# A perceiver layer with routed tokens and experts on one core: ranks and counts of the token sort moved into the batches, the planner's clock in its last steps, and pairs of states added in the last scan

## The chip, the core and the metric

The kernel runs on one core of one Trainium2 chip. The metric is the time on the device in microseconds (us), the median of several runs. TensorE (PE, with its weight loads shown apart as PEld), VectorE (DVE), ScalarE (ACT), GpSimd (POOL) and SyncE (SP, which only issues transfers here) each execute their own queue in the order in which the program issues it; they wait for one another by semaphores. All data are float32.

## The reference, cut to what matters

B = 4 batches of T = 256 tokens with D = 256 features are the state x; each batch has a context of S = 4096 rows. Three parts are added to x one after the other:

```python
x = x + cross_attention(layernorm(x), ctx)     # 8 heads of 64; keys: the context and the tokens themselves
x = x + token_router(layernorm(x))             # see below
x = x + experts(layernorm(x))                  # 8 experts, 2 for each token

# token router, for each batch
scores = gelu(xn @ r_w1 + r_b1) @ r_w2 + r_b2
top 64 of 256 tokens  -> a small attention among them
other 192, in order   -> a state space scan: 512 channels, 16 states
    h[t] = dA[t] * h[t-1] + dBu[t];   y[t] = sum over 16 states of h[t] * C[t]

# experts
routing = softmax(xf @ router_w.T); the two largest, divided by their sum, weigh
out = sum over the two experts e of  w_e * ((silu(x @ gate_e) * (x @ up_e)) @ down_e)
```

So the experts of a batch's tokens are known only when that batch's scan has ended, and the scan of a batch needs that batch's cross attention.

## The kernel before

**Cross attention** fills the first 1264 us. It runs in N = 128 steps, 32 for a batch, and two further turns of the loop drain it (`for n in range(N + 2)`, from L1406). A group G is two heads of one batch, eight steps. In a step, PE multiplies the scores `su` (`scores`, L1247 to L1261); VectorE copies them out with their maximum (`copy_max`, L1273, L1280) and finds the common bound `nb` after a small product (`stat`, L1285, L1290); ACT takes the exponentials of the step before (`exps`, L1301); VectorE transposes these (`turn`, L1310, two a step, for the two heads). Every four steps PE multiplies the transposed blocks with the values (`values`, L1319, `po`), which have to wait for the last of the four pairs of transposes. The keys and values of the next group, `psk` (L1200) and `psv` (L1237), are multiplied in between as "pieces". The last pieces of a group's own tokens (`psv` again) and the output projection `psx` (`project`, L1366), added to x on VectorE (L1374), end each batch. The last steps have no pieces: there is no next group.

**The planner.** The program text is executed once, when the kernel is built, and writes out each engine's queue. Work that is not attention lies in background generators. `slot(budget)` is called at fixed places of a step; it lets every active generator that is due by the clock `now[0]`, and whose announced cost fits into what is left of the budget, go on to its next `yield due, cost`. The clock is an estimate: it moves by fixed amounts as pieces and scores are issued.

```python
def slot(budget):
    room[0] = budget
    for item in list(active):
        if item[1] <= now[0] and item[2] <= room[0]:
            room[0] -= item[2]
            step(item)
```

A smaller first number after `yield` lets the generator be continued at an earlier slot; the costs are guesses of VectorE's time.

**The background** is, for each batch after its attention (`routed`): router, small attention (`attention`; its softmax yields at L429), the scan's preparation, the scan, `ssm_back` (sums, output product `pssd`, `psback` that puts the rows in place). For batches 0, 1 and 2 `ssm_scan` runs beside the attention of the batch that follows, with POOL taking part of it. Then `sortable(b)` (L841 to L880) normalizes the batch's tokens: moments on VectorE, `x4` on ACT (L851), a transfer to `x4d` in memory (L855), four transposes `psx4` on PE (L863), copies `x4T` on ACT (L869), the logits `pslg` on PE (L874), and their copy to `lgs` on VectorE (L878).

After batch 2, `dispatch` (L907 to L1027) sorts the 768 tokens of the first three batches (NSORT = 6 tiles of 128) to their experts, all at once: `ranks` (L882 to L890) finds each expert's place among a token's eight logits by comparing all with all; `weights_of` (L892 to L905) has the marks of the two chosen ones, an exponential on ACT, and the two weights; a running sum over the six tiles (L936 to L938); three matmuls `pscnt` that count over partitions (L943 to L949); the number of blocks of 128 for each expert and where they begin (L954 to L960); each token's `slots` (L967 to L973) and `weights` in one loop; `experts`, the expert of each of the NB = 19 blocks (L977 to L982); each token's block and place in it (L991 to L995); then the comparisons `inb` (L1003, L1006) and `at` (L1012), 12 x 2 products `pstok` on PE (L1022) and the cast to `tokens` (L1026), the list of rows that each block gathers. In the queues, these operations stand among the operations of the last steps of the attention.

**The expert stage.** `ordered` runs the 19 blocks: for block j an indirect transfer on POOL's queue gathers the 128 rows of x4d that `tokens` names (`gather`, L1567), the expert's three matrices are loaded on SP's queue by the number in `experts` (`load`, L1529), PE transposes the rows (`turn_block`, L1579, copied by ACT at L1582) and multiplies gate and up (`half`, p0b and p1b, L1588), ACT takes a tanh and VectorE gates (`gated`, L1538 to L1543: `sg`, `hb`), PE multiplies down (`pdb`, L1602), and the rows go to `ysd` in memory (L1610). The pools of gathered rows and of expert weights lie in the memory that the attention used before. Beside these blocks run router, small attention and scan of the last batch, batch 3. Its scan is `ssm_scan_late` (L677 to L751): 16 parts of 4 states x 128 channels x 192 tokens. For each part ACT computes four decays, VectorE multiplies (L738), scans (L739) and multiplies by C (L745), and PE adds the four states by four products with the identity, accumulated in one bank `yps` (`sums`, L711 to L717):

```python
def sums(i):
    k, m = divmod(i, NDT)
    for s in range(SG):                       # SG = 4
        nc.tensor.matmul(
            yps[:, m // 2, (m % 2) * NBOT : (m % 2 + 1) * NBOT], ident, dbl[i][:, s, :],
            start=False, stop=(k == K - 1 and m % 2 == 1 and s == SG - 1),
        )
```

`ssm_back` (L754) and `prepare` (L1661) end that batch's routing; `collect` gathers the experts' rows of the first three batches and adds them with the `weights`; and the last batch goes through all eight experts densely (`experts`, pg and pu L1719, pde L1732).

Of the kernel before, what the change touches and what calls it, by code (L numbers as in the profile page):

```python
# [8 lines left out]
F32 = mybir.dt.float32  # L9
# [37 lines left out]
def perceiver_layer(ctx: ExitStack, tc: tile.TileContext, a: dict, out: bass.AP):  # L47
# [311 lines left out]
    def attention(b, st):  # L359
# [69 lines left out]
        yield 2.5, 0.9  # L429
# [248 lines left out]
    def ssm_scan_late(b, st):  # L678
# [32 lines left out]
        def sums(i):  # L711
            k, m = divmod(i, NDT)
            for s in range(SG):
                nc.tensor.matmul(
                    yps[:, m // 2, (m % 2) * NBOT : (m % 2 + 1) * NBOT], ident, dbl[i][:, s, :],
                    start=False, stop=(k == K - 1 and m % 2 == 1 and s == SG - 1),
                )  # L717
# [16 lines left out]
        for i in range(K * NDT):  # L734
# [10 lines left out]
            nc.vector.tensor_tensor(db, db, spread[k, 1], ALU.mult)  # L745
            if i:
                sums(i - 1)
# [80 lines left out]
    lgs = bg.tile([P, NSORT, E], F32, name="lgs")  # L828
# [12 lines left out]
    def sortable(b):  # L841

        yield 1.5, 1.2
# [14 lines left out]
        yield 2.5, 0  # L858
# [13 lines left out]
        for t in range(2):  # L872
# [5 lines left out]
        nc.vector.tensor_copy(  # L878
            lgs[:, 2 * b : 2 * b + 2, :].rearrange("p t e -> p (t e)"), ps[:, : 2 * E]
        )  # L880
# [26 lines left out]
    def dispatch():  # L907

        n = NSORT
        yield 1.7, 1.1  # L910
        gt, eq = scratch(0, [P, n, E, E], "gt"), scratch(1, [P, n, E, E], "eq")
        parts = [scratch(i, [P, 2 * DS * DTR * 3 // 4], "part") for i in range(2)]
        used = [0, 0]
# [13 lines left out]
        rk, comb, two = carve(0, n, E), carve(0, n, E), carve(0, n, E)  # L927
        mx, sm = carve(0, n), carve(0, n)
        for _ in ranks(lgs, n, rk, gt, eq):
            yield 1.0, 1.3  # L930
        yield 1.0, 1.0
        w = weights_of(lgs, rk, comb, two, mx, sm)
        next(w)

        prev = carve(0, n + 1, E)
        nc.vector.memset(prev[:, 0, :], 0.0)  # L936
        for t in range(n):
            nc.vector.tensor_tensor(prev[:, t + 1, :], prev[:, t, :], two[:, t, :], ALU.add)  # L938
        yield 2.0, 1.0
        next(w, None)  # L940
        ps = bank("pscnt")
        cnt, num = ps[:, : n * E], ps[:, n * E : (n + 1) * E]
        nc.tensor.matmul(  # L943
            cnt, cs["tri"], two.rearrange("p t e -> p (t e)"), start=True, stop=False
        )
        nc.tensor.matmul(
            cnt, ones, prev[:, :n, :].rearrange("p t e -> p (t e)"), start=False, stop=True
        )
        nc.tensor.matmul(num, ones, prev[:, n, :], start=True, stop=True)  # L949
        yield 1.7, 1.1  # L950

        full, nblk = carve(0, E, n), carve(0, E)
        bb, sb = carve(1, E, E), carve(0, E)
# [3 lines left out]
        nc.vector.tensor_reduce(out=sb, in_=bb, axis=AX.X, op=ALU.add)  # L957

# [5 lines left out]
        mine, sl = carve(1, 2, n, E), carve(0, 2, n)  # L964
        for dst, src in ((sl, slot), (order["weights"], comb)):
            for k in range(2):
                nc.vector.scalar_tensor_tensor(  # L967
                    out=mine[:, k], in0=rk, scalar=float(k), in1=src,
# [3 lines left out]
            if src is slot:  # L972
                nc.vector.tensor_copy(order["slots"], sl.rearrange("p k t -> p (k t)"))  # L973
                yield 1.0, 1.0

        end, past, eb = carve(0, E), carve(1, NB, E), carve(1, NB)
        nc.vector.tensor_tensor(end, sb, nblk, ALU.add)  # L977
        nc.vector.tensor_tensor(
            past[:1], bc(end[:1], 1, NB), bc(cs["iblk"][:1], 2, E), ALU.is_le
        )  # L980
        nc.vector.tensor_reduce(out=eb[:1], in_=past[:1], axis=AX.X, op=ALU.add)
        nc.vector.tensor_scalar(  # L982
            out=order["experts"], in0=eb[:1], scalar1=float(E - 1), scalar2=None, op0=ALU.min
        )
# [25 lines left out]
        for i, tag in enumerate(("ua", "permT", "dsort")):  # L1010
# [6 lines left out]
            if i == 1:  # L1017
                yield 1.0, 0.7
# [783 lines left out]
```

## Time and profile before

| | us |
|---|---|
| median of 3 runs (1548.88 to 1555.13) | 1551.75 |
| the profiled execution | 1554.27 |
| its span in the trace | 1552.5 |
| PE busy | 1468.3 (95% of the span) |
| PEld busy | 1048.7 (68%) |
| DVE busy | 1045.3 (67%) |
| ACT busy | 757.0 (49%) |
| POOL busy | 410.0 (26%) |

The mean clock granted to PE is 0.979 of full; 223.40 MB are moved, 144 GB/s on the mean. By stages, the busy times are (from the trace cut into stretches):

| stretch, us | what | length | PE | DVE | ACT | granted clock |
|---|---|---|---|---|---|---|
| 586 to 893 | middle of the attention | 307.0 | 299.4 | 232.5 | 174.1 | 1.00 |
| 1200 to 1264 | last steps of the attention, dispatch | 64.0 | 49.7 | 42.0 | 20.5 | 0.87 |
| 1264 to 1350 | first blocks, router of batch 3 | 86.0 | 71.3 | 28.1 | 35.3 | 0.88 |
| 1350 to 1457 | blocks, last scan, its output | 107.0 | 98.9 | 76.8 | 37.6 | 0.97 |
| 1457 to 1552 | experts of the last batch | 95.0 | 86.7 | 44.3 | 15.7 | 0.98 |

How to read such a profile: the span is the time from the first to the last instruction of the execution; the time of a run is a little longer. "Busy" counts an engine's instructions and not its waits. A line L1310 is line 1310 of the kernel. In groups and timelines, `pt<-sp` means a tile pt written from a tile sp, then shapes, the number of instructions, and in brackets the idle time of the engine before it and the instruction that ended that wait. A wait printed as `PE x L1 <- DMA y: 4.7, 3, 2.5` lists the total, the number and the longest. The chain of waits follows the last instruction back to what released it, step by step.

### The profile page before, as it was taken

The page shows a single profiled execution, that of the slowest core. Times are in us where ns is not written, and L with a number is a line of the kernel's source. Part 1 is how long each engine was busy: PE and PEld are TensorE (multiplying, and loading weights), DVE is VectorE, ACT ScalarE, POOL GpSimd, SP SyncE. Part 2 cuts the span into 40 slices and gives each one's busy share as a digit, 9 for nine tenths or more (in the row PEclk, how much of TensorE's full clock was granted, in tenths as well). Part 3 has the DMA queues.
Part 4 walks back from the last instruction along what each step waited for, and adds up shares of the span by engine and source line. Part 5 has one row for each costly group of instructions (what it writes and reads, how often), then busy time and mean ns, then how long its engine had stood idle before and what let it go on. Part 6 is the DMA issues. An engine that isn't in the chain of part 4 may idle for free.

```text
span 1552.5 us, 37355 instructions
## 1 busy us (share of the span) xinstructions
PE 1468.3 (95%) x15748; PEld 1048.7 (68%) x15748; DVE 1045.3 (67%) x1771; ACT 757.0 (49%) x1483; POOL 410.0 (26%) x464
## 2 busy tenths in 40 slices
PE   7999999999999899999999999999998779799899
PEld 3757667576667475776665667756666558688787
DVE  1666666666599976565999755758987644477453
ACT  3444454464566644545667454556654422534211
POOL 1000000000089940000799500006995011010110
PEclk9999999999999999999999999999999969999999
DMA  7445543524344525243454343335543144667562
GB/s 235 155 131 160 164 142 101 180 75 141 116 149 142 178 87 189 82 141 109 141 171 160 110 154 116 108 113 156 166 130 107 37 139 128 230 218 244 157 208 83
DMA packets 157766, 223.40 MB, mean 144 GB/s; under 512 B 14976, under 2 KB 76160, under 8 KB 157600
## 3 DMA queue, kind: packets, MB, share of 16 engines
q1 hardware_dynamic: 152368, 211.45, 42.5%
q10 hardware_dynamic: 3744, 5.51, 1.1%
q0 software_dynamic: 1488, 4.07, 1.0%
q8 instruction: 124, 2.03, 0.5%
q14 instruction: 42, 0.34, 0.1%
HBM read 216.56 MB, written 4.42 MB: 142 GB/s over the span
## 4 chain that ended last, share of the span: by engine, by line
PE 67%; POOL 14%; DVE 10%; issue 4%; ACT 2%; DMA 2%; ACTq 0%; SPq 0%; DVEq 0%; POOLq 0%
PE po L1319 12%; PE su L1253 11%; PE psv L1237 11%; PE psk L1200 10%; POOL y L652 5%; POOL db L637 5%; POOL db L650 4%; DVE sp L1273 4%; PE su L1261 2%; PE pg L1719 2%; PE pde L1732 2%; PE pu L1719 2%; PE p0b L1588 2%; PE p1b L1588 2%; DVE db L644 1%
## 5 line engine op out<-in xcount | busy, mean ns | idle before, releaser
L1273 DVE TENSOR_SCALAR_CACHE_REDUCE sp<-su 128x1088 f32<-128x1088 f32 x256 | 318.8, 1281 | 182.0 <-PE su L1261 182.0
L1310 DVE STREAM_TRANSPOSE pt<-sp 128x1088 f32<-128x1088 f32 x256 | 328.0, 1296 | 62.8 <-PE po L1319 62.6
L1301 ACT ACTIVATE sp<-sp,nb 128x1088 f32<-128x1088 f32 x256 | 305.2, 1196 | 10.6 <-DVE nb L1290 10.4
L1319 PE MATMUL po<-pt,v 128*64 128x128 f32 x4352 | 261.7, 277 | 1.3 <-DVE pt L1310 1.3
L1253 PE MATMUL su<-kt,qz 64*32 64x512 f32 x4096 | 255.1, 607 | 4.3 <-DVE nb L1290 3.5
L1200 PE MATMUL psk<-ctx,wk 128*128 128x512 f32 x512 | 246.3, 614 | 8.9 <-DMA ctx<-in_ctxT 6.4
L1237 PE MATMUL psv<-wv,ctx 128*128 128x128 f32 x2048 | 250.3, 279 | 0.2
L1319 PEld LDWEIGHTS po<-pt,v 128*64 128x64 f32 x4352 | 240.0, 138 | 12.8 <-issue 7.5
L1237 PEld LDWEIGHTS psv<-wv,ctx 128*128 128x128 f32 x2048 | 236.1, 192 | 6.3 <-issue 1.5
L1200 PEld LDWEIGHTS psk<-ctx,wk 128*128 128x128 f32 x512 | 91.7, 192 | 93.9 <-issue 86.7
L1188 ACT COPY kt<-psk 128x512 f32<-128x512 f32 x128 | 74.8, 585 | 158.5 <-PE psk L1200 158.3
L1253 PEld LDWEIGHTS su<-kt,qz 64*32 64x32 f32 x4096 | 63.2, 107 | 123.5 <-issue 93.3
L652 POOL TENSOR_TENSOR y<-y,db 128x192 f32<-128x192 f32 x192 | 135.0, 703 | 15.1
L1241 ACT COPY v<-psv 128x512 f32<-128x512 f32 x144 | 78.9, 558 | 118.4 <-PE psv L1237 117.2
L644 DVE TENSOR_TENSOR_SCAN db<-da,db 128x384 f32<-128x384 f32 x96 | 123.2, 1283 | 14.4 <-POOL db L637 3.7
L650 POOL TENSOR_TENSOR db<-db,cb 128x384 f32<-128x384 f32 x96 | 110.5, 1152 | 26.4 <-DVE da L642 26.4
L395 POOL TENSOR_TENSOR kbd<-qk,hmask 128x512 f32<-128x512 f32 x8 | 8.2, 1044 | 407.6 <-ACT qk L385 407.6
L637 POOL TENSOR_TENSOR db<-bb,xc 128x384 f32<-128x384 f32 x96 | 111.0, 1178 | 0.2
L1261 PEld LDWEIGHTS su<-kt,qz 128*32 128x32 f32 x2048 | 34.7, 110 | 109.3 <-issue 109.3
L632 ACT ACTIVATE da<-delta,A_log_sb 128x192 f32<-128x192 f32 x192 | 75.4, 447 | 51.5 <-DVE da L642 39.1
L1356 ACT COPY ao<-po 128x128 f32<-128x128 f32 x32 | 8.5, 264 | 165.5 <-PE po L1319 165.5
L1285 PEld LDWEIGHTS su<-mq,same 128*128 128x128 f32 x256 | 40.7, 190 | 53.6 <-DVE mq L1280 36.3
(277 smaller groups left out, 1594.0 us busy)
## 6 DMA issues: line engine op xcount, KB each, us to landing
ctx<-in_ctxT SPq DMA_DIRECT2D x256, 512.0 KB, 4.8
gateT<-in_gateT SPq DMA_DIRECT2D x27, 512.0 KB, 4.0
upT<-in_upT SPq DMA_DIRECT2D x27, 512.0 KB, 5.3
downT<-in_downT SPq DMA_DIRECT2D x27, 512.0 KB, 6.2
bb<-bcd SPq DMA_DIRECT2D x24, 192.0 KB, 4.1
cb<-bcd SPq DMA_DIRECT2D x24, 192.0 KB, 3.6
wv<-in_wv SPq DMA_DIRECT2D x32, 128.0 KB, 2.4
in_w<-in_in_w SPq DMA_DIRECT2D x32, 128.0 KB, 3.9
```

The source lines that it names most:

```text
L637: nc.gpsimd.tensor_tensor(db, bbs[k], bc(xc[:, m, :], 1, SG), ALU.mult)
L644: nc.vector.tensor_tensor_scan(out=db, data0=da, data1=db, initial=0.0, op0=ALU.mult, op1=ALU.add,)
L650: nc.gpsimd.tensor_tensor(db, db, cbs[k], ALU.mult)
L652: nc.gpsimd.tensor_tensor(y[:, m, :], y[:, m, :], db[:, s, :], ALU.add)
L1200: nc.tensor.matmul(ps, wqk[G][:, 0, c, :], ct[:, c, :], start=(c == 0), stop=(c == KD - 1),)
L1237: nc.tensor.matmul(ps[:, i * P : (i + 1) * P], lhsT, wv[G][:, w, c, :], start=(c == 0), stop=(c == KD - 1),)
L1241: nc.scalar.copy(v.rearrange("p k d -> p (k d)"), ps[:, : n * P])
L1253: nc.tensor.matmul(su[q * 32 : (q + 1) * 32, SC[j] + lo : SC[j] + lo + 512], qT[r, j, s * 32 : (s + 1) * 32], kt[r, q, lo : lo + 512], sta ...
L1273: nc.vector.tensor_scalar(out=sps[n][j], in0=su[:, SU[j] : SU[j] + QK], scalar1=1.0, scalar2=None, op0=ALU.mult, op1=ALU.max, accum_out=nm ...
L1301: nc.scalar.activation(sps[n][j], sps[n][j], AF.Exp, bias=nbs[n][:, j : j + 1], accum_out=lss[b][:, hp, s, j : j + 1],)
L1310: nc.vector.transpose(pts[m, j][:, i, :], sps[n][j])
L1319: nc.tensor.matmul(pos[m][j * HD : (j + 1) * HD, :], vts[m // 2, k // 4][:, k % 4, j * HD : (j + 1) * HD], pts[m, j][:, :, kk * 32 : (kk + ...
```

## The change

Four things are changed.

1. *Ranks, weights and counts by batch.* `sortable(b)` no longer keeps the logits; after the logits' product it copies them, ranks them, marks the chosen two, takes the exponential on ACT and adds the marks to the running sum `upto`, for its two tiles alone, at one slot. The rest of the weights follows at another slot for batches 0 and 1 and is left for later for batch 2. `dispatch` begins with the count products, now four of them.
2. *The order in dispatch.* The blocks' experts are found directly after the counts, ahead of the slots; the three comparisons `at` each have a slot; the weights of batch 2 and the choice of all `weights` come last, after `tokens`.
3. *The planner.* Due times are changed at four places (1.5 to 1.0, 2.5 to 1.7, 2.5 to 4.0 and those of dispatch). In the last steps (`tail`) the clock also moves for the pieces that are missing there, and one slot's budget is 1.3 instead of 0.5.
4. *The last scan.* VectorE adds the two pairs of states of a part in one further operation (128 x 384 elements), and `sums` has two products a part instead of four.

```diff
@@ attention
-        yield 2.5, 0.9
+        yield 4.0, 0.9
@@ ssm_scan_late
         def sums(i):
             k, m = divmod(i, NDT)
-            for s in range(SG):
+            for s in range(SG // 2):
                 nc.tensor.matmul(
                     yps[:, m // 2, (m % 2) * NBOT : (m % 2 + 1) * NBOT], ident, dbl[i][:, s, :],
-                    start=False, stop=(k == K - 1 and m % 2 == 1 and s == SG - 1),
+                    start=False, stop=(k == K - 1 and m % 2 == 1 and s == SG // 2 - 1),
                 )
...
             nc.vector.tensor_tensor(db, db, spread[k, 1], ALU.mult)
+            nc.vector.tensor_tensor(db[:, : SG // 2], db[:, : SG // 2], db[:, SG // 2 :], ALU.add)
             if i:
                 sums(i - 1)
@@ sortable
-        yield 1.5, 1.2
+        yield 1.0, 1.2
...
-        yield 2.5, 0
+        yield 1.7, 0
         ps = bank("psx4")
...
-        nc.vector.tensor_copy(
-            lgs[:, 2 * b : 2 * b + 2, :].rearrange("p t e -> p (t e)"), ps[:, : 2 * E]
-        )
+        yield 1.0, 1.25
+
+        part, used = scratch(0, [P, 384], "part"), 0
...
+        nc.vector.tensor_copy(lg, ps[:, : 2 * E])
...
+        for _ in ranks(lg, 2, rks[:, tiles], gt, eq):
+            pass
+        w = weights_of(lg, rks[:, tiles], combs[:, tiles], twos[:, tiles], mx, sm)
+        next(w)
+        for t in range(2 * b, 2 * b + 2):
+            if t:
+                nc.vector.tensor_tensor(
+                    upto[:, t, :], upto[:, t - 1, :], twos[:, t, :], ALU.add
+                )
+            else:
+                nc.vector.tensor_copy(upto[:, 0, :], twos[:, 0, :])
+        if b < B - 2:
+            yield 1.7, 1.0
+            next(w, None)
+        else:
+            order["weigh"] = w
@@ dispatch
-        for _ in ranks(lgs, n, rk, gt, eq):
-            yield 1.0, 1.3
-        yield 1.0, 1.0
-        w = weights_of(lgs, rk, comb, two, mx, sm)
-        next(w)
...
+        yield 1.7, 0
+
         ps = bank("pscnt")
         cnt, num = ps[:, : n * E], ps[:, n * E : (n + 1) * E]
+        for t0, t1, last in ((0, 1, True), (1, n, False)):
+            nc.tensor.matmul(
+                cnt[:, t0 * E : t1 * E], cs["tri"],
+                twos[:, t0:t1].rearrange("p t e -> p (t e)"), start=True, stop=last,
+            )
         nc.tensor.matmul(
...
+            cnt[:, E:], ones, upto[:, : n - 1].rearrange("p t e -> p (t e)"),
+            start=False, stop=True,
+        )
+        nc.tensor.matmul(num, ones, upto[:, n - 1, :], start=True, stop=True)
+        yield 1.7, 1.25
...
+        nc.vector.tensor_reduce(out=eb[:1], in_=past, axis=AX.X, op=ALU.add)
+        nc.vector.tensor_scalar(
+            out=order["experts"], in0=eb[:1], scalar1=float(E - 1), scalar2=None, op0=ALU.min
+        )
+
         slot = carve(0, n, E)
...
+        yield 1.0, 1.25
+        chosen(sl, slot)
+        nc.vector.tensor_copy(order["slots"], sl.rearrange("p k t -> p (k t)"))
...
-        yield 1.0, 1.2
-
+        yield 1.0, 1.25
+
...
-        yield 1.0, 1.3
 
         ats = []
         for i, tag in enumerate(("ua", "permT", "dsort")):
+            yield 1.0, 0.7
             at = bg.tile([P, 4, P], F32, tag=tag, name="at")
...
             ats.append(at)
-            if i == 1:
-                yield 1.0, 0.7
         yield 1.5, 0.2
         ps = bank("pstok")
...
         nc.vector.tensor_copy(order["tokens"], ps[:, :NB])
         order["ready"] = True
+        yield 1.0, 1.25
+        next(order["weigh"], None)
+        chosen(order["weights"], combs)
@@ main loop
+                tail = n >= N - 2
+
                 def piece(i):
                     if i < len(pieces):
                         pieces[i]()
+                    if i < len(pieces) or tail:
                         now[0] += took
...
-                    slot(0.5)
+                    slot(1.3 if tail else 0.5)
```

`chosen(dst, src)` is the former loop over slots and weights as a function: for k = 0, 1 it multiplies (rank equal to k) with src and sums over the experts.

## The prediction

> **What bounds the kernel now.** I read the page's chain first, then the stretches of ten microseconds over the end, then the chain in order of time and the waits of each stage.
>
> ```profile
> PE 67%; POOL 14%; DVE 10%; issue 4%; ACT 2%; DMA 2%; ACTq 0%; SPq 0%; DVEq 0%; POOLq 0%
> ```
>
> The page has PE busy 95% of the span, and PE holds 67% of the chain. Between 586 and 893 us the waits of PE add up to 7.4 us, so there its order decides. The end is another stage:
>
> ```profile
> 1220.00:1230.00 10.00, 8.95 (x156) 7.01 (x155) 6.50 (x13) 2.64 (x5) 0.00 (x0) 1.00 0.01 3
> 1230.00:1240.00 10.00, 5.46 (x55) 2.28 (x55) 6.56 (x19) 2.72 (x5) 0.00 (x0) 0.66 0.00 1
> 1240.00:1250.00 10.00, 2.76 (x19) 2.04 (x20) 9.24 (x22) 2.48 (x4) 0.00 (x0) 0.66 0.00 0
> 1250.00:1260.00 10.00, 9.49 (x82) 7.72 (x78) 5.74 (x22) 0.00 (x0) 0.00 (x0) 0.82 0.01 2
> 1260.00:1270.00 10.00, 8.05 (x93) 7.29 (x93) 2.83 (x11) 3.29 (x7) 0.77 (x1) 0.86 0.49 165
> 1270.00:1280.00 10.00, 6.70 (x24) 5.03 (x25) 0.00 (x0) 3.96 (x7) 5.30 (x7) 0.50 1.05 365
> ```
>
> Columns: stretch, length, busy time of PE, PEld, DVE, ACT, POOL, granted clock, DMA share, GB/s. From 1230 to 1250 VectorE (15.8 of 20 us) sets the pace and PE is idle or at half clock; from 1270 PE waits for transfers. The timeline shows what opens the expert stage:
>
> ```profile
> 1263.81 0.40 SPq L1529 DMA_DIRECT2D gateT<-in_gateT  x1
> ...
> 1268.18 0.18 DVE L1026 CAST tokens<-pstok 128x19 int32<-128x19 f32 x1 [0.88 <-PE pstok L1022]
> ...
> 1269.23 1.12 POOL L1567 DMA_INDIRECT xg<-x4d,tokens  x1 [78.22 <-DMA upT<-in_upT]
> ...
> 1276.82 3.79 PE L1588 MATMUL p0b<-xTb,gateT 128*128 128x128 f32 x16 [0.46 <-ACT xTb L1582]
> ```
>
> The last value product ends at 1263.77 (T below). The experts were known at 1252.5, yet the weights start at T: their memory is the attention's. Only the gather is later, by 5.4 us, because of the tokens. Then the scan stage:
>
> ```profile
> PE p0b L1588 <- DMA gateT<-in_gateT: 4.7, 3, 2.5
> PE yps L714 <- DVE db L745: 2.9, 3, 2.0
> ```
> ```profile
> DVE sg L1539 <- ACT sg L1538: 19.9, 8, 5.9
> ```
> ```profile
> 1368.16 0.95 DVE L738 TENSOR_TENSOR db<-bbl,xc 128x768 f32<-128x768 f32 x1
> 1369.15 1.76 DVE L739 TENSOR_TENSOR_SCAN db<-dal,db 128x768 f32<-128x768 f32 x1
> 1370.94 0.96 DVE L745 TENSOR_TENSOR db<-db,cbl 128x768 f32<-128x768 f32 x1
> 1371.82 0.95 DVE L738 TENSOR_TENSOR db<-bbl,xc 128x768 f32<-128x768 f32 x1
> ```
>
> Waits of 1349 to 1457 (PE) and 1349 to 1446 (VectorE): total, times, longest. PE has 7.6 us of large waits in 100 us, VectorE 19.9. So the last scan is PE's, and VectorE has 20 us to give; one scan costs it 3.66 us (1368.16 to 1371.82).
>
> **A. Up to the last value product.** The built order of the changed kernel shows what moves.
> A1. In steps 61, 93 and 125 the transposes psx now stand ahead of the own-token products psv (1.14 us). These filled PE's wait for ACT's first x; now PE waits there (1212.8 to 1213.7), waits 0.70 for the second x as before, and runs psv after it. The next scores start 1.0 later: +3.0 in all; 0 if other waits swallow it, of which there is little.
> A2. VectorE's rank work per batch has 15 to 17 operations. The 128x128 ones are not in the trace: between 0.23 (128x64, L956) and 0.56 (128x384, L885); I take 0.30, nearer the smaller. Five of them and ten or so at 0.17 to 0.25 make some 4 us where VectorE now sits idle 3.54 us (before L1310 at 597.26) in steps 61 and 93; the rest fits in the 0.29 that it waits for scores after: 0.
> A3. In step 125 the counts (pscnt) stand inside the value products and wait for the ranks: PE is there at 1225.1, the last sum of counts is ready at about 1226.1, and four matmuls cost about 1.0 (eight passes like L874's, 1.06). Before, three of them cost 1.19 at 1239.1, hidden behind scores. Now +1.5, because the next transposes (L1310) wait for the last of these products.
> A4. In step 126 VectorE does nine small operations ahead of nb (L954 to L960, 1.18, and L977 to L982, 0.95: 2.13) instead of 1.68: +0.45. Ten more (0.73 + 1.0 + 0.9 = 2.65) follow the second transpose and fit into its 3.16 us wait for scores: 0; uncovered they would cost their 2.65. In step 127 one equality (0.68, L1012) replaces five operations (1.03): -0.25.
> A5. Still in step 127, after nb: two equalities (1.3), then the token cast stands ahead of the last two transposes and waits for pstok. With nb at 1246.9 (2.7 late by A1 for one step, A3, A4), the equalities end at 1249.5; the last 16 of 24 passes take 1.5 at full clock (3.15 for 24 in the trace) or about 3 at half; cast, two transposes and two small operations 3.4. The last transpose ends at 1254.5 to 1255.6, against 1249.0: +2.8 to +3.9 more, taken as 3.2. Queued behind the cast are exactly the transposes that the value products wait for. SP's load of the experts moves up a step and still waits for T.
> A6. The products of step 129 run 4.10 us for 34 at half clock, 2.12 for 36 at full. With pstok just before, some may be at full: 0 to -2, taken as -0.5.
> Sum A: 3.0 + 1.5 + 0.45 - 0.25 + 3.2 - 0.5 = **+7.4**.
>
> Row first: the granted clock fell to 0.50 about 1234 and 1244, after some 4 us in which PE did 0.4 us of work, and was back at 1253.2, 4 us after dense work began. [...]
>
> For the ranks, 128x384 takes 0.56 and 128x48 0.20, so width hardly pays at this size. [...]
>
> **B. From T to the first late scan** (db at 1350.81, T + 87.0). Gather and weights now start together. With the 6.33 us that the gather took under the same load it lands at T + 6.4; nearest other row 3.8, the median. ACT's queue holds the router's scaling until T + 6.3. Transposes 0.7 and copy 0.4: p0b at T + 7.5 instead of T + 13.05, cold 3.79. On PE then psxn, p1b, psh, a second block's 3.57, pssc at 18.6 (hT by ACT, with two table loads of 1.28, at 18.3), pdb 1.73 to T + 21.0. VectorE's ranking starts at 19.2 and takes 2.9 + 1.4 (a gate pair) + 1.5 + 0.2: psn at T + 25.3, where it is now. PE idles 4.3 there, goes cold as at 1291 and does block 2 in 5.4: psg at T + 31.4 (now 30.6). So the chain comes no earlier; PE is some 4.4 us of block work ahead, and pstok's 3.15 are gone. In the built order from psg to pspr are 23.4 us of PE work: pspr ends at T + 56.3 (now 55.9).
> From there to the first db it is 31.2 now: L586 waits 11.4, because VectorE reaches L568 only after a gate that waits for ACT. In the new order that gate comes before ACT's wait for the bcd transfer. ACT is free at 8.1 and does L586 to 9.4; psdt, psas and softmax put ln at 19.1, tanh of a block at 21.4; VectorE's gate, L431, delta, xc and oa end at 26.1. First db at T + 82.5: **-4.5**; 0 to -8.
>
> **C. The scans.** PE loses 16 times two matmuls, 16 x 0.65 = 10.4 us (1.30 for the four, from the chain). VectorE gains 16 additions of 128x384: 0.56 (L885), between 0.48 (start to start) and 0.96 (768 wide); with 0.06 for waiting on the product, 0.62. VectorE from first db to last addition: 16 x 4.28 + 11 gate pairs x 1.39 + 0.45 = 84.2, against 91.0 elapsed now. PE in the same stretch: 11.4 blocks x 5.52 + 16 x 0.65 = 73.3, plus waits. VectorE becomes the bound; with 3.0 for its waits (transfers of 4.7 on PE, half absorbed): 87.2, **-3.8**.
> **D. After it.** Now 15.1 from the last product (1441.85) to the end of psback (1456.96), with 12.6 of PE work left over. In the new order two of the matmuls of the last sum and six of pdb are left; the gate pair, two y, zs (3.5 us on VectorE), pssd, its copies and psback end at +10.0: **-5.0**. Expert stage for the last batch (95.5 us): 0, the collecting operation that VectorE now does inside prepare costs 0.1.
>
> Sum: 7.4 - 4.5 - 3.8 - 5.0 = -5.9. The profiled execution took 1554.27 (span 1552.5 and 1.8 around), 2.5 above the median of the runs shown, 1551.75; the same -5.9 from the median gives **1546**.
>
> **Rivals.** Forecast, 1541 to 1551: chance 0.45.
> Rival 1, no queue cost in steps 125 to 129: pstok and the products run at full clock and A1 is swallowed, A = +2: -11.3, 1540 (1536 to 1543). For: the scores end late in step 127, so the clock may hold. Against: PE's 3.3 us at 1240.3 were enough to lose it. 0.22.
> Rival 2, the gather is hidden anyway: the router's ranking decides, and L586's gain goes into another wait of ACT: B = 0, -1.4, 1550 (1548 to 1553). 0.16.
> Rival 3, slower: VectorE's 19.9 us of waits in the scan are latency that stays (a gate needs PE's p1b and ACT's tanh in series), so the additions come on top: C = 16 x 0.62 = +9.9 instead of -3.8, +7.8, 1560 (1553 to 1566). It decides once the waits for sg stay above some 13 us. For: single waits of 5.9 and 3.9. Against: both follow waits of PE for gateT. 0.17.
> That the change does not do what it says is out: the built order has the tokens two steps earlier and two matmuls a sum.
>
> **Numbers.** Range 1538 to 1559: it leaves out the far ends of rivals 1 and 3 and takes in the bounds of A5 and B. A measurement of this kernel can tell 0.5% (7.8 us) from no change. Faster by more (under 1544): rival 1 and a third of the forecast, 0.37. Slower (over 1559.5): two thirds of rival 3 and a little, 0.13. Within: 0.50.
>
> **What would show it.** A: the last value product at 1269 to 1273 instead of 1263.8, and a wait of VectorE for pstok in step 128; without this wait A5 is wrong. B: first gather within 0.2 us of the first gateT, p0b about 7.5 after T, psn still 25 after T, first db near T + 82. C: 20 us of waits for sg shrink to a few, and PE waits for db at many yps. D: 10 from the last addition to psback's end. Wrong altogether if T does not move, or if VectorE still waits 15 us for ACT in the scan.

## The result and the profile after

| | before | after |
|---|---|---|
| median, us (20 runs each) | 1554.8 | 1554.73 |
| after / before | | 0.9995 (95%: 0.9984 to 1.0006) |
| span of the profiled execution, us | 1552.5 | 1553.9 |
| PE busy | 1468.3 (95%) | 1461.9 (94%) |
| DVE busy | 1045.3 (67%) | 1057.1 (68%) |

The change makes no difference that can be measured: -0.8 us, between -2.5 and +0.9. It is not that nothing happened. Line numbers of after are 26 to 30 higher behind `dispatch`. The page's chain of after:

```profile
PE 63%; POOL 14%; DVE 13%; issue 4%; ACT 3%; DMA 2%; ACTq 0%; SPq 0%; DVEq 0%; POOLq 0%
```

PE has lost 4% of the chain, and VectorE has gained 3. By stages, worked out from the timelines of the profiled executions (T is the end of the last value product; "bound 124" the bound nb of step 124, L1290, now L1316):

| us | start to bound 124 | to T | T to first db | first db to end of psback | to the first pg | to the end |
|---|---|---|---|---|---|---|
| before | 1213.1 | 50.7 | 87.0 | 106.2 | 5.2 | 90.3 |
| after | 1215.5 | 58.6 | 82.6 | 96.2 | 9.6 | 91.4 |
| difference | +2.4 | +8.0 | -4.4 | -10.0 | +4.4 | +1.1 |

The stages moved by up to 10 us and cancel to +1.4, the difference of the two spans. These are single executions. First the end of the attention, in stretches of ten microseconds (columns as in the prediction):

```profile
1230.00:1240.00 10.00, 4.24 (x80) 2.34 (x82) 8.52 (x19) 2.92 (x6) 0.00 (x0) 0.77 0.01 2
1240.00:1250.00 10.00, 6.40 (x58) 3.14 (x42) 9.05 (x21) 3.52 (x7) 0.00 (x0) 0.50 0.00 0
1250.00:1260.00 10.00, 7.23 (x48) 6.69 (x50) 5.41 (x15) 1.16 (x2) 0.00 (x0) 0.50 0.01 2
1260.00:1270.00 10.00, 9.48 (x63) 7.62 (x60) 0.71 (x2) 0.00 (x0) 0.00 (x0) 0.69 0.00 0
```

VectorE is busy 17.6 of the 20 us from 1230 on, and PE's clock is at half from 1240 to 1260, where it was 0.66 and 0.82 before. The timeline of after names the operations:

```profile
1250.43 3.60 PE L1045 MATMUL pstok<-eq,at 128*128 128x19 f32 x16 [1.10 <-DVE at L1037]
...
1254.07 0.18 DVE L1049 CAST tokens<-pstok 128x19 int32<-128x19 f32 x1 [3.09 <-PE pstok L1045]
...
1257.28 4.10 PE L1345 MATMUL po<-pt,v 128*64 128x128 f32 x34 [1.06 <-DVE combs L931]
...
1274.15 0.40 SPq L1559 DMA_DIRECT2D gateT<-in_gateT  x1
...
1274.41 1.12 POOL L1597 DMA_INDIRECT xg<-x4d,tokens  x1 [81.08 <-PE po L1345]
...
1280.96 3.78 PE L1618 MATMUL p0b<-xTb,gateT 128*128 128x128 f32 x16 [0.46 <-ACT xTb L1612]
```

VectorE waits 3.09 us for pstok with two transposes behind the cast; T is 1274.1 instead of 1263.8. The gather now starts with the first weights, and the first block's products start 6.85 us after T, not 13.05. The largest waits of the scan stage, 1356.7 to 1452.9, PE and then VectorE:

```profile
PE yps L714 <- DVE db L746: 7.8, 10, 1.6
PE p0b L1618 <- ACT xTb L1612: 2.4, 2, 1.6
```
```profile
DVE sg L1569 <- ACT sg L1568: 1.4, 2, 0.7
```

VectorE's 19.9 us of waits have shrunk to 1.4, and PE waits for VectorE ten times: the bound has changed sides. At the end of that stage stands something new (timeline of after):

```profile
1454.87 0.30 ACT L194 ACTIVATE rs<-mv,eps_t 128x2 f32<-128x2 f32 x1 [2.28 <-DVE mv L184]
...
1456.17 0.95 POOL L1672 DMA_INDIRECT yg<-ysd,slots  x1 [49.84 <-DMA ysd<-yb]
...
1458.92 0.48 DVE L1680 SCALAR_TENSOR_TENSOR x_sb<-yg,eweights,x_sb 128x256 f32<-128x256 f32 x1 [4.08 <-DMA yg<-ysd,slots]
1459.32 0.16 DVE L201 RECIPROCAL rs<-rs 128x2 f32<-128x2 f32 x1
...
1462.49 2.07 PE L1749 MATMUL pg<-x4Tl,gateT 128*128 128x256 f32 x4 [0.68 <-ACT x4Tl L1709]
```

psback ends at 1452.9 instead of 1457.0. ScalarE has the last batch's scales at 1455.2, but their reciprocal stands in VectorE's queue behind the first adding of gathered rows, L1680, and VectorE waits there 4.08 us for the gather. So pg, the first product of the last experts, starts at 1462.5; before, it started at 1462.2.

### The profile page after: what moved, and what is told of

It reads as the page before. It is cut to its first block, busy times and chain, and to the rows that moved or that the text cites. A ratio compares the mean times of both kernels' runs of the same rounds, so it can differ in the third digit from the quotient of the medians.

```text
span 1553.9 us, 37283 instructions
## 1 busy us (share of the span) xinstructions
PE 1461.9 (94%) x15686; PEld 1039.5 (67%) x15686; DVE 1057.1 (68%) x1812; ACT 758.9 (49%) x1486; POOL 412.0 (27%) x464
## 4 chain that ended last, share of the span: by engine, by line
PE 63%; POOL 14%; DVE 13%; issue 4%; ACT 3%; DMA 2%; ACTq 0%; SPq 0%; DVEq 0%; POOLq 0%
PE po L1345 12%; PE su L1279 11%; PE psv L1263 11%; PE psk L1226 9%; POOL y L652 5%; POOL db L637 5%; POOL db L650 4%; DVE sp L1299 4%; PE su L1287 2%; PE pg L1749 2%; PE pu L1749 2%; PE pde L1762 2%; DVE pt L1336 2%; DVE db L739 1%; DVE db L644 1%
## 5 line engine op out<-in xcount | busy, mean ns | idle before, releaser
L1226 PEld LDWEIGHTS psk<-ctx,wk 128*128 128x128 f32 x512 | 91.4, 191 | 94.3 <-issue 85.0
L652 POOL TENSOR_TENSOR y<-y,db 128x192 f32<-128x192 f32 x192 | 135.2, 704 | 15.1
```

The costliest lines, as they stand in the source:

```text
L652: nc.gpsimd.tensor_tensor(y[:, m, :], y[:, m, :], db[:, s, :], ALU.add)
L1226: nc.tensor.matmul(ps, wqk[G][:, 0, c, :], ct[:, c, :], start=(c == 0), stop=(c == KD - 1),)
```

## The experiments

All times are medians; the ratio is to the kernel before, run on the same chip, whose median lay between 1554.6 and 1555.8 us. Each kernel starts from the changed one unless said otherwise.

| kernel | us | ratio (95%) |
|---|---|---|
| e1_collect_late | 1550.79 | 0.9983 (0.9971 to 0.9996) |
| e2_cast_late | 1556.79 | 1.0011 (1.0000 to 1.0023) |
| e3_pairs_only | 1549.47 | 0.9970 (0.9958 to 0.9982) |
| e4_no_pairs | 1552.23 | 0.9992 (0.9980 to 1.0003) |
| e5_psv_first | 1547.25 | 0.9953 (0.9935 to 0.9972) |
| e6_psl_first | 1550.81 | 0.9973 (0.9960 to 0.9985) |
| e7_three | 1543.06 | 0.9921 (0.9903 to 0.9938) |
| e8_three_no_pairs | 1540.13 | 0.9904 (0.9887 to 0.9921) |
| e9_half_pairs | 1537.93 | 0.9888 (0.9866 to 0.9911) |
| e10_pairs_pool | 1543.86 | 0.9926 (0.9904 to 0.9949) |
| e11_no_pairs_again | 1540.47 | 0.9906 (0.9882 to 0.9930) |
| e12_store_queue | 1552.09 | 0.9982 (0.9967 to 0.9997) |

### e1: the adding of gathered rows held back

```diff
                 if i < 2 * n:
                     ... gather ...
+                while i == 2 and "x4T" not in dense:
+                    yield 1.0, 0
                 if i >= 2:
                     ... L1680 ...
```

> The changed kernel, but VectorE's first adding of gathered expert rows (L1680) waits in the planner until the last batch's transposed tokens exist; the gathers themselves stay where they are. Theory (a new wait ate the gain): in the changed kernel VectorE stood 4.08 us in front of L1680 for the gather, with the last batch's reciprocal (L201) queued behind it, and the first products pg and pu after it ran at a lower clock, about 1 us. So pg starts some 4 to 5 us sooner after psback, and the time falls by 4 to 5.5 us against the changed kernel, to about 1550. Rival (the stage is held by something else, such as the experts' weights or ScalarE): pg starts at the same distance from psback, 9.6 us, and the time stays at 1554.7.

Measured: 1550.79 us. The end of its scan stage:

```profile
1456.04 0.69 DVE L784 TENSOR_TENSOR x_sb<-x_sb,psback 128x512 f32<-128x512 f32 x1 [6.57 <-PE psback L779]
...
1458.31 0.17 DVE L201 RECIPROCAL rs<-rs 128x2 f32<-128x2 f32 x1 [0.36 <-ACT rs L194]
...
1461.13 2.07 PE L1749 MATMUL pg<-x4Tl,gateT 128*128 128x256 f32 x4 [0.68 <-ACT x4Tl L1709]
...
1461.44 0.48 DVE L1682 SCALAR_TENSOR_TENSOR x_sb<-yg,eweights,x_sb 128x256 f32<-128x256 f32 x1 [2.77 <-DMA yg<-ysd,slots]
```

The reciprocal follows ScalarE by 0.36 us, VectorE waits for the gather after it, and pg starts 5.1 us after psback, as before the change. The new wait is shown. In the median it is worth 3.9 us, by the ratios 1.9; the interval of the ratio still overlaps that of the changed kernel.

### e2 and e6: what holds the last transposes

e2 moves the cast alone (`yield 0.5, 0.2` ahead of it):

> The changed kernel, but the cast of pstok to tokens (one VectorE operation of 0.18 us) is one slot later, behind the last two transposes instead of ahead of them; no other instruction moves. Theory (VectorE's queue holds up the last transposes): in the changed kernel VectorE waited 3.09 us for pstok with two transposes behind the cast. Now the last transpose ends near 1253.7 instead of 1257.2, the last value product comes 2.7 us sooner at an unchanged clock, and up to 1.8 us more if the full clock comes back before the last 36 products of the pair that ran 4.00 us; the time falls by 2.7 to 4.5 us, to about 1551. Rival (PE's pstok at half clock, 3.60 us, is what the products wait for): the transposes come sooner but the products do not, less than 1 us.

Measured: 1556.79 us, no gain; the theory fell, and the rival holds in part. The timeline of e2:

```profile
1257.40 0.20 DVE L1364 RECIPROCAL rl<-psl 64x8 f32<-64x8 f32 x1 [2.12 <-PE psl L1359]
...
1275.06 1.13 POOL L1597 DMA_INDIRECT xg<-x4d,tokens  x1 [80.14 <-DVE ao L1388]
...
1282.21 0.66 PE L1609 MATMUL psxb<-ident,xg 128*128 128x128 f32 x2 [6.64 <-DMA xg<-x4d,tokens]
```

Without the cast it is the reciprocal L1364 that waits, 2.12 us: it needs psl, and psl stands behind pstok on PE. From the bound of step 127 to the end of the last transpose it takes 7.7 us instead of 8.8, and to T 22.6 instead of 25.6, because in this profile half of the products that follow also ran at full clock again. What is won there is lost behind T: the gather starts 0.9 us after T instead of 0.3. POOL's wait for the last value product now stands on an instruction of its own ahead of the gather: that wait ends at 1274.23, the gather starts 0.83 later. Its data then need 7.2 us instead of 5.5 beside the weights. T to the first db grows from 82.6 to 86.8. So e6 moves four of the twelve products too, and gives the first four gathers memory that is free before T:

```diff
         for i in range(2 * n):
+            if i == 8:
+                yield 1.0, 0.2
             nc.tensor.matmul(ps[:, :NB], ats[i // 4][:, i % 4], inb[:, i], ...
...
-                    xgs[j] = fp.tile([P, D], F32, tag="xg", name="xg", bufs=4)
+                    if j < 4:
+                        if j % 2 == 0:
+                            xgs["own"] = bg.tile([P, 2, D], F32, tag=("ua", "permT")[j // 2], name="xg")
+                        xgs[j] = xgs["own"][:, j % 2, :]
+                    else:
+                        xgs[j] = fp.tile([P, D], F32, tag="xg", name="xg", bufs=4)
```

> The changed kernel with the last four of the twelve products pstok, and the cast to tokens, one slot later: PE does psl between them, and VectorE's cast stands behind the last two transposes. The first four gathered blocks get memory that the attention doesn't use, so that their gathers need only tokens. Theory (what held the last transpose when the cast was moved was the reciprocal L1364, which waits for psl, which stood behind pstok on PE): nb of step 127 to the end of the last transpose takes about 5.9 us instead of 8.8 in the changed kernel and 7.7 with the cast alone moved, the last value product comes 2.8 us sooner, the first block's products start within 7 us of it (9.15 with the cast alone moved), and the time falls by 3 us, to about 1552. Rival 1 (the products wait for PE's own pstok at half clock): the transposes end sooner, the last value product doesn't, 0 to 1 us. Rival 2 (the first blocks are bound by the experts' weights): the early gathers change nothing after the last value product, T to the first db stays at 82.6.

Measured: 1550.81 us, 3.9 less than the changed kernel, as the theory has it. Its timeline:

```profile
1254.02 0.28 PE L1359 MATMUL psl<-ls,same 128*32 128x8 f32 x4
1254.23 1.90 PE L1047 MATMUL pstok<-eq,at 128*128 128x19 f32 x8
1254.37 0.20 DVE L1364 RECIPROCAL rl<-psl 64x8 f32<-64x8 f32 x1 [0.41 <-PE psl L1359]
...
1256.63 1.13 POOL L1602 DMA_INDIRECT xg<-x4d,tokens  x1 [60.89 <-DVE part L932]
```

The last transpose ends 6.0 us after the bound of step 127. The gather runs 16 us ahead of T and moves T to the first db by only 0.6 (82.0), so with the gather no later than the weights, the transfer of rows is not what binds the first block. There ScalarE copies the block's rows (xTb, 1279.10) 4.3 us after PE has transposed them, behind the router's scaling in its queue.

### e3 and e4: the pairs alone, and all but the pairs

e3 is the kernel before with the edits in `ssm_scan_late`, e4 the changed kernel without them.

> The kernel before with the pairs of states added on VectorE alone (16 additions more, 32 matmuls less); ranks, dispatch and planner as before. Theory (VectorE becomes the bound of the scan, and what PE saves is spent at the end on products that are left over): the scan from the first product on VectorE to the last one's end takes 86 to 87 us instead of 91.0, and the 12.6 us of block work that stand in PE's queue behind the last sums stay, so the time falls by about 4.6 us, to 1550. Rival 1 (all of the saved PE time counts): 9 to 10 us less, 1545. Rival 2 (the waits of VectorE are latency that stays, and the additions come on top): 3 to 10 us more.

> The changed kernel with the pairs undone: four matmuls a part, no addition on VectorE; ranks, dispatch and planner as changed. Theory (the attention's end costs 10.3 us, the earlier start of the experts gives 4.4 of them back, the scan is bound by PE again): the last value product stays near 1274 and the first db near T + 82.5, the scan and its output take about 4 us longer than in the changed kernel, and the wait for the gather ahead of the last experts stays: about 1558.5. Rival (the pairs are worth nothing in this order because VectorE becomes the bound): 1554.7.

Measured: e3 1549.47 us, as the theory had it in size; by stages 3.1 of the 5.0 us come from the scan (87.9 from its first product to its last operation, not 86 to 87) and 1.9 from the work behind it, which the theory left as it was. e4 1552.23 us, 6 us below the theory: the rival holds in the time, though without the pairs it is PE that binds. From the first db to the end of psback, one row for each kernel, in the order before, e3, e4, after (stretch, length, busy time of PE, PEld, DVE, ACT, POOL, clock, DMA):

```profile
1350.81:1456.96 106.15, 98.08 (x655) 91.72 (x653) 76.09 (x77) 36.74 (x96) 7.21 (x7) 0.97 0.73 237
```
```profile
1345.68:1446.85 101.17, 87.41 (x591) 79.69 (x589) 84.74 (x93) 36.60 (x96) 8.25 (x7) 0.98 0.77 248
```
```profile
1354.01:1449.59 95.58, 93.50 (x635) 86.39 (x635) 76.13 (x77) 38.34 (x102) 7.61 (x7) 1.00 0.78 254
```
```profile
1356.71:1452.90 96.19, 85.43 (x572) 75.86 (x571) 84.61 (x93) 38.48 (x102) 9.26 (x7) 1.00 0.79 253
```

The pairs alone take 5.0 us from this stretch (106.2 to 101.2), the rest of the change alone takes 10.6 (95.6), both together take 10.0 (96.2). With the new order PE is busy 93.5 of 95.6 us: the waits for weights that the kernel before had (4.7 us for gateT) are gone, and PE has 22 block products (p0b, p1b) fewer here because it did them earlier. The pairs then take 8.1 us off PE and put 8.5 on VectorE, and VectorE binds at the same length. Both parts of the change relieve PE; with both in, VectorE binds in its place, and the second part gains nothing.

### e5: the order of the x4 transposes

One due time is as before: `yield 2.5, 0` instead of `yield 1.7, 0` ahead of psx4.

> The changed kernel with one due time as before (2.5 instead of 1.7 ahead of psx4): in steps 61, 93 and 125 the four own-token products psv stand ahead of the four transposes psx4 again; no other matmul moves. Theory (the transposes wait for ScalarE and psv behind them can't fill the wait): the bound nb of steps 61, 93 and 125 moved by 0.83 to 0.85 us against the kernel before at just these three steps; undone, the time falls by 2.5 us, to about 1552. Rival (other waits of VectorE or ScalarE take the place): the shift of 0.85 us stays in the steps after, and the time stays at 1554.7.

Measured: 1547.25 us, 7.5 less than the changed kernel, by the ratios 6.5 (0.9953 against 0.9995). The bounds of steps 61, 93 and 125 come 0.84 us sooner each, 2.5 in all; that much was expected. More came from the clock. In step 74 the six profiled kernels with psx4 ahead took 16.35 to 16.37 us from bound to bound, the eight with psv ahead all 14.75; in step 106 the six took 16.35 to 16.37 again, and six of the eight 14.75 (in step 42 it is the other way: one of six took the longer time against four of eight). In step 74, after and then before:

```profile
722.75 0.66 PE L437 MATMUL psat<-ident,pa 128*128 128x128 f32 x4 [1.45 <-ACT ev L586]
723.33 3.13 PE L1345 MATMUL po<-pt,v 128*64 128x128 f32 x28
```
```profile
722.84 0.65 PE L437 MATMUL psat<-ident,pa 128*128 128x128 f32 x4 [1.45 <-ACT ev L586]
723.42 1.75 PE L1319 MATMUL po<-pt,v 128*64 128x128 f32 x28
```

The same wait of 1.45 us, and then the same 28 products: 3.13 us against 1.75. In the clock records of these profiles every change lies on a grid of 3.41 us; the half clock of after lasts one step of it here, from 723.50 to 726.91. The stretch with the wait and the one that follows, in after and then in before:

```profile
720.09:723.50 3.41, 1.96 (x20) 1.33 (x17) 0.00 (x0) 1.42 (x5) 0.00 (x0) 1.00 0.00 0
723.50:726.91 3.41, 3.41 (x36) 2.79 (x42) 0.42 (x1) 0.90 (x3) 0.00 (x0) 0.50 0.00 0
```
```profile
721.05:724.46 3.41, 1.96 (x26) 1.50 (x26) 0.00 (x0) 1.94 (x5) 0.00 (x0) 1.00 0.00 0
724.46:727.88 3.42, 3.42 (x66) 1.77 (x63) 2.68 (x4) 2.64 (x5) 0.00 (x0) 1.00 0.00 0
```

PE was busy for 1.96 of 3.41 us in both, and only in after does half clock follow, so the busy share does not decide here. What goes with it is the place of the wait in its stretch. The same wait stands in steps 42, 74 and 106, so the fourteen profiles have it 42 times. Half clock followed all 19 times that it ended 1.9 to 3.3 us after the start of a stretch or within 0.1 us of the start of the next, and none of the 23 times that it ended 0.3 to 1.8 us after the start. In step 74 it ended 0.6 to 1.8 us after the start in the eight with psv ahead, and 2.0 to 3.2 in the six with psx4 ahead. By the counts of these steps, of 1.6 us each, the clock gives e5 some 2 us on the mean beside the 2.5, an estimate; the rest of the 6.5 is not accounted for, and the 6.5 are known to some 3 us only.

### e7 and e8: three edits together, with and without the pairs

e7 has the edits of e1, e5 and e6; e8 takes the pairs out as well.

> The changed kernel with three edits together: psv ahead of psx4 again, psl ahead of the last pstok with early gathers, and VectorE's first adding of gathered expert rows held back until the last batch's transposed tokens exist. Theory (the three losses are in series and independent): 2.5 + 2.8 + 4.5 to 5.5, about 10 us less than the changed kernel, 1545. Rival (they hide one another): no better than the best of the three alone, 1550.

> The same three edits, and the pairs of states undone (four matmuls a part). Theory (in the changed order VectorE bounds the last scan, so the pairs are worth nothing, as without the three edits, where the stretch from the first db to the end of psback took 95.6 us without the pairs and 96.2 with them): the same as with the pairs within 1 us, about 1545. Rival (with the waits at its end gone, PE bounds the scan again): 3 to 5 us more than with the pairs.

Measured: 1543.06 and 1540.13 us. By the ratios e7 is 11.5 us below the changed kernel, and the three alone add up to 11.8 (1.9 + 6.5 + 3.4), as the theory has it for losses in series that do not hide one another; each of these numbers is known to some 3 us only. The stretch from the first db to psback takes 96.7 us with the pairs and 95.9 without. By the ratios e8 is 2.6 us below e7, with intervals that overlap; the rival, 3 to 5 us more without the pairs, is out.

### e9, e10 and e11: where the pairs belong

e9 adds pairs in every second part, e10 all on GpSimd, e11 is e8 again.

```diff
 e9:
+            n = SG // 2 if i % 2 else SG
-            for s in range(SG // 2):
+            for s in range(n):
...
+            if i % 2:
                 nc.vector.tensor_tensor(db[:, : SG // 2], db[:, : SG // 2], db[:, SG // 2 :], ALU.add)
 e10:
-            nc.vector.tensor_tensor(db[:, : SG // 2], ...
+            nc.gpsimd.tensor_tensor(db[:, : SG // 2], ...
```

> The three edits again, with the pairs added on VectorE in every second part of the last scan only: 8 additions, and 48 matmuls yps instead of 64 without or 32 with all pairs (counting one for each state or pair). Theory (from the first db to the end of psback PE is the bound without the pairs, busy 93.5 of 95.6 us, and VectorE with them, PE busy 85.4 of 96.2 us; so the best lies between): the stretch takes 92 to 93 us, and the time is 2 to 3 us below the kernel with the three edits and no pairs, about 1537. Rival (what stands between is the chain of a gate, tanh on ScalarE and two operations on VectorE, in series with both): 95 to 96 us as in both, and the same time, 1540.

> The three edits again, with all 16 additions of pairs on GpSimd instead of VectorE. Theory (PE loses about 8 us of busy time as with the pairs on VectorE, and VectorE keeps its queue): from the first db to the end of psback 89 to 91 us instead of 95.9 without pairs, and the time 5 us below it, about 1535. Rival 1 (GpSimd and VectorE slow each other: the scan of 128x384 beside a busy GpSimd took 1.28 us, that of 128x768 alone 1.76): the operations L738 to L745 get longer by a fifth or more, and the stretch takes 96 us or more. Rival 2 (GpSimd's addition is late: 128x384 took it 1.15 us): PE waits for it at each sum, 93 to 95 us.

> The kernel with the three edits and no pairs once more, on the same chip as the two others, for a comparison side by side: 95.9 us from the first db to the end of psback, 1540 us by both theories.

Measured: 1537.93, 1543.86 and 1540.47 us. The same stretch in e9:

```profile
1347.59:1440.99 93.40, 89.41 (x604) 81.04 (x603) 80.36 (x85) 38.35 (x102) 9.05 (x7) 1.00 0.79 261
```

PE 89.4 and VectorE 80.4 of 93.4 us: the load is shared, and the stretch is 2.2 us shorter than in e11 (95.57). The time says the same, 2.5 us, though the intervals overlap. e10's theory fell: its stretch takes 100.1 us. PE's waits there, and GpSimd's addition:

```profile
PE yps L714 <- POOL db L746: 9.2, 9, 2.8
```
```profile
L746 POOL TENSOR_TENSOR db<-db x16: 992/999/1573, 1350.0 to 1435.5; 128x384 f32<-128x384 f32 x16
```

Rival 1 was right in kind and too large in size. Where GpSimd's addition and a scan of VectorE overlapped, in four of the sixteen parts, both were longer: the scan took 2.36 us instead of 1.76, the addition 1.57 instead of 1.00. The first of the four:

```profile
1361.12 1.57 POOL L746 TENSOR_TENSOR db<-db 128x384 f32<-128x384 f32 x1 [3.30 <-DVE db L745]
1361.95 2.36 DVE L739 TENSOR_TENSOR_SCAN db<-dal,db 128x768 f32<-128x768 f32 x1
```

VectorE's multiplications beside the addition kept their 0.95 us. L738 to L745 took 2.4 us more in all, 4% and not a fifth. The addition alone takes 1.0 us instead of 0.56, and PE waits 9.2 us for it; VectorE's waits for ScalarE's tanh, behind PE, are 11.1 us. Rival 2 had the mechanism of these waits, but the stretch is 5 to 7 us longer than it said. Of that, PE's own work is 3.2 us longer than with the pairs on VectorE (88.6 against 85.4), since the clock was 0.97 in the mean of this stretch and not 1.00.

### e12: the last store on another queue

> The changed kernel, but the last block's store of its rows (ysd, 128 KB) is issued on ScalarE's queue instead of SP's. Theory (in the changed kernel SP issued that store at 1447.31 behind three transfers of 512 KB, and the first gather started 8.9 us later, at 1456.17; the wait of VectorE at L1680 is the wait for this store): the first gather starts within 4 us of the store, VectorE no longer waits 4.08 us at L1680, pg starts 5 to 6 us after psback instead of 9.6, and the time falls as with the adding held back, by 2 to 5 us, to about 1551. Rival (the DMA engines are full with the weights whichever queue the store is on): the gather starts as late, pg stays at 8.5 to 9.6 us after psback, and the time at 1554.7.

Measured: 1552.09 us. The timeline of e12:

```profile
1445.68 0.33 ACTq L1640 DMA_DIRECT2D ysd<-yb  x1
...
1453.12 0.94 POOL L1672 DMA_INDIRECT yg<-ysd,slots  x1 [48.21 <-DMA downT<-in_downT]
...
1455.91 0.48 DVE L1680 SCALAR_TENSOR_TENSOR x_sb<-yg,eweights,x_sb 128x256 f32<-128x256 f32 x1 [2.50 <-DMA yg<-ysd,slots]
```

The gather starts 7.4 us after the store instead of 8.9, and VectorE still waits 2.50 us; pg comes 8.0 us after psback. Other profiles of kernels with this wait have 8.4 to 9.6, so the queue is worth little. What the gather waits for is the landing of the store itself. Its row in the list of transfers (queue, size, us from issue to landing), in after and then in e12:

```profile
ysd<-yb SPq DMA_DIRECT2D x1, 128.0 KB, 8.0
```
```profile
ysd<-yb ACTq DMA_DIRECT2D x1, 128.0 KB, 6.5
```

The gather starts 0.9 us after that in both. Before the change the same store took 1.8 us, when all but the end of the weights had landed; now it is issued among 1.5 MB of them. So the rival holds: either queue is slow here.

## Why the prediction was wrong

The forecast was -5.9 us; measured were -0.8, between -2.5 and +0.9. The forecast gain was not there. That 1554.73 lies in the range of 1538 to 1559 is in part luck: the forecast stood on 1551.75, the median of three runs, and twenty runs of the kernel before gave 1554.8, so -5.9 would have been 1548.9. Point by point, in the profiled executions:

- **The step that failed: the last batch's experts**, "0, the collecting operation that VectorE now does inside prepare costs 0.1". Measured +5.5 us from psback to the end (101.0 against 95.5). I had seen the operation move into prepare and priced it at 0.1; what it waits for, a gather of rows that are stored behind the weights, was not asked. With the wait taken out, in e1, this stretch takes 95.4 again. The 5.5 belong to this execution: the five other profiles that keep the wait (e2, e4, e5, e6, e12) have 98.3 to 99.3, so 2.8 to 3.8 more than before.
- **A, sum +7.4.** T came 10.3 later. A1: 0.84 in each of three steps, as worked out (2.5 instead of 3.0), but not the clock that it costs in other steps (e5). A2: 0, right; that no 128x128 rank operation is in the trace was a mistake, L885 at 1470.41 took 0.29, and 0.30 was the value taken. The rows for 48 and 384 columns (0.20 and 0.56), from which I had that width hardly pays, say that it does, 8 times the columns in 2.8 times the time; the fifteen rank operations of 128x128 take 4.3 us in after, where five of 128x384 took 2.8. A3 and A4: +1.57 between the bounds of steps 125 and 126 and -0.45 to that of 127, for 1.95 and -0.25. A5: +3.8 for 3.2, but the cast was not the only thing: take it away, and a reciprocal that waits for PE's psl stands there (e2, e6). A6, taken as -0.5, was +2.2 in this execution: the second 36 products took 4.00 us at half clock where they had taken 2.19. From the last transpose to T it was 16.9 us here, against 14.7 before. Of the eleven other profiles with the changed order e6 has 16.9 too and ten have 13.8 to 14.9, one of them (e7) with the edits of e6, so A6 varies and the order does not settle it. The last 0.7 of the 10.3 lie ahead of bound 124, where step 74 took 1.6 more and step 42 1.6 less.
- **B, -4.5.** Measured -4.4: first block 6.85 after T (7.5), psn 26 (25.3), first db 82.6 (82.5). e2 shows how narrow it is: with the gather 0.6 us later, first db is 86.8 after T, and nearly all of it is lost.
- **C and D, -3.8 and -5.0.** Measured -4.7 and -5.3, with VectorE as the bound and 86.35 us from the first db to the last addition (87.2). The sizes were right and the cause was not: I put C down to the 10.4 us of products that the pairs save. e4 has the whole gain without the pairs: 84.2 us from the first db to the last product and 11.4 from there to the end of psback, where it was 91.0 and 15.1 before.
- **Rivals.** Rival 1 (T only 2 later) is out, T was later than the forecast. PE's 3.3 us that it names stand ahead of 1245.7; at 1240.3 PE waited 1.72. Rival 2 (B = 0) is out by B. Rival 3 (VectorE's waits stay) is out: 1.4 us of them are left.

The sum as measured: 10.3 - 4.4 - 4.7 - 5.3 + 5.5 = +1.4, the difference of the spans.

## What to carry to other kernels

An operation that moves ahead of another in a queue costs what it waits for, not what it lasts (here 4.08 us for an operation of 0.48): ask for each one that is newly in front of something urgent when its input lands, above all when that input is a transfer of data that a faster stage now delivers only just in time. Two edits that relieve the same engine need not add (5.0 and 10.6 us of the last scan's stretch alone, 10.0 together): work out which engine binds when the first is in, and split work between two engines until both are nearly full (e9) rather than move all of it. A planner that only knows costs of operations will place a late arrival in front of the chain; a condition on what must be ready first (e1) costs two lines. The best kernel here, e9, is 1.1% (0.9 to 1.3%) below the kernel before, which the changed one equals; it keeps the changed order, adds pairs in every second part, and has three side effects taken out.

## What the hardware showed that I had not expected

- In the clock records of the fourteen profiled executions every change of PE's granted clock lies on a grid of 3.41 us. I counted their 6,041 stretches at full clock by the share of time in which PE was busy: under 43%, the next stretch was at half clock 99 times in 100; between 43 and 60%, 39 times in 117; over 60%, 3 times in 5,824 (in before and after alone 17 of 17, 7 of 20 and 1 of 827). In step 74 of after a wait of 1.45 us was followed by half clock and cost 1.4 us of products (3.13 against 1.75). Between 43 and 60% the share alone does not tell: one and the same wait, with PE busy for 1.96 of 3.41 us, was followed by half clock when it ended 2.67 us after the start of its stretch (after) and not when it ended 1.79 us after it (before; e5 has the other steps).
- So a change in the order of eight small products, which shifts what follows by 0.84 us at three steps, moved the time by 6.5 us by the ratios (some 3 either way), of which only 2.5 are the shift itself.
- In e2, with a wait on an instruction of its own ahead of a gather, instead of on the gather, the gather started 0.6 us later (0.9 after T, not 0.3), and its rows came 2.3 us later, with the weights on the way at the same time. The first gather of ysd, whose last wait stands on such an instruction in before and after, starts 0.7 us behind it in both (1457.55 to 1458.24, 1455.48 to 1456.17); the first gather of x4d in after, which waits itself, starts 0.3 us after its release (T, 1274.1, to 1274.41).
